# State-space scan on Trainium2: the first state of three scans in four is carried by ScalarE in place of a pointer

## The chip, the cores and the metric

The kernel runs on one core of a Trainium2 chip. The metric is the device time of one execution in microseconds (us). A core has five engines that run side by side, each with a queue of its own that it works off in order: TensorE (PE in the profile; its weight loads are PEld), VectorE (DVE), ScalarE (ACT), GpSimd (POOL) and SyncE (SP), which here only issues DMAs. An engine waits for another through semaphores, and while an instruction waits, everything behind it in that queue waits too.

## The reference

There are two layers. The first is a Mamba block over 4 images of 128 channels and 128 x 128 pixels, read as sequences of 16384 tokens. A small MLP and a projection give 256 inner channels, a causal convolution and SiLU give `u`, and then the selective scan runs over the sequence with 16 states for each channel:

```
delta = softplus(dt @ dt_proj_w.T + dt_proj_b)
A = -exp(A_log)
def step(h, inp):
    d_t, B_t, C_t, u_t = inp
    dA = exp(d_t[:, :, None] * A)
    h = h * dA + d_t[:, :, None] * B_t[:, None, :] * u_t[:, :, None]
    y = einsum('bds,bs->bd', h, C_t)
    return (h, y)
_, ys = scan(step, h0, xs)          # h0 = 0
y = ys + u * D
y = y * silu(z)
```

An output projection, a group norm, SiLU and a residual follow. The second layer normalizes the result, forms four weights for each image, and filters the image in the frequency domain (real FFTs as products with constant matrices).

## The kernel before

`block0` is the first layer and takes nine tenths of the time. The four images are cut into 128 chunks of T = 512 tokens, 32 an image (`NCH`). Of a chunk, 256 channels x 16 states are 4096 recurrences of 512 steps. They are laid on the 128 partitions as 32 tiles of 128 x 512: two halves of the channels (`j`), four rounds of states (`r`), and four places (`p`). I call the four tiles of one (`j`, `r`) a group; a chunk has eight groups (`u`), and two slots for each, 16 slots a chunk (`NP`). Slot 2u has places 0 and 1 of its group, slot 2u+1 places 2 and 3.

For each tile the work is:

- ScalarE: `da = exp(delta * A)` (`exps`, line 393). The result of place 0 lies in SBUF in two buffers, that of places 1, 2 and 3 in one PSUM bank each, so the next group's exponential of a place has to wait until VectorE is done with this one's.
- GpSimd: `hb = du * B` for places 1 to 3 (`dbu`, line 363), issued two slots ahead. For place 0, TensorE transposes a product of ScalarE into PSUM (`b0`, line 383).
- VectorE: the scan `h = da * h + b` over 512 steps (`scans`, line 412). Its first state is a constant 0 in the first chunk of an image; otherwise it is read through a pointer, a [128,1] column `st` that holds the last state of the chunk before.
- h*C: for places 2 and 3 VectorE multiplies (line 414), and ScalarE then copies the last column to `st` (line 415). For places 0 and 1 GpSimd multiplies (line 419), and ScalarE copies the last columns one slot later (phase "late", reported as line 554). `by_vector` has the exceptions: one tile more goes to VectorE in odd chunks, one less in "norming" chunks.
- TensorE: the sum over states into `y` (`sums`, line 433).

The order is written out by hand. Every step is put into a list under a slot and a phase (`todo`), and a loop over slots and phases issues them, so that each engine's queue follows the order of the phases. In one odd slot, ScalarE's queue is: place 1's exponential, the late state copy, the chunk's other work (phase "act"), the early exponential of place 0 of the group after, and the state copies of the scans. In the even slot it is: the exponentials of places 2 and 3, then other work. That other work is the preparation of the next chunks: Relu, copies, SiLU with a table load at slot 2 (lines 242 and 239), softplus with two table loads at slot 6 (line 275), the scaling of `bt` (line 304), and so on.

From image 1 on, the work of finishing the image before is spread over the chunks: chunks 2 to 17 of an image (`norming`) normalize (lines 633, 637 and 641), the later ones form the aggregation (line 667), and `spectrum` computes parts of the FFT ahead of time in some chunks. `spectrum` has one-buffer tiles: `fx` for the loaded rows, `fs` between the two products and `fq` for the stored result.

`block1` is the second layer. The change doesn't touch it.

Of the kernel before, what the change touches and what calls it, by code (L numbers as in the profile page):

```python
# [26 lines left out]
F32 = mybir.dt.float32  # L27
AF = mybir.ActivationFunctionType
# [5 lines left out]
P = 128  # L34
# [3 lines left out]
NP = 16  # L38
# [8 lines left out]
def kernel(ctx: ExitStack, tc: tile.TileContext, a: dict, out: bass.AP):  # L47
# [101 lines left out]
    spec = [dpool.tile([H, C, 2, WF], F32, tag=f"spec_{b}", name=f"spec_{b}") for b in range(EARLY)]  # L149
    shared = SimpleNamespace(**{k: v for k, v in locals().items() if k not in ("ctx", "tc")})  # L150
    block0(tc, shared)
    block1(tc, shared)


def block0(tc, s):
    nc, B, NCH, NH, NS, NG, ND, R, NX, KC, HALO, C, L, NF, DI = (
        s.nc, s.B, s.NCH, s.NH, s.NS, s.NG, s.ND, s.R, s.NX, s.KC, s.HALO, s.C, s.L, s.NF, s.DI,
    )
    NT = T // P
    with ExitStack() as ctx:  # L160
        def pool(name, bufs, **kw):
            return ctx.enter_context(tc.tile_pool(name=name, bufs=bufs, **kw))

        p1 = pool("p1", 1)
        p2 = pool("p2", 2)
        hpool = pool("hb", 4)
        tiny = pool("tiny", 2)
# [13 lines left out]
        st = {}  # L181
# [156 lines left out]
        def norming(k):  # L338

            return k >= NCH and 2 <= k % NCH < 2 + NCH // 2  # L340

        def place(r, p):


            return (p - r) % ND

        def by_vector(k, j, r, p):

            if norming(k):
                return p > 1 and (j, r, p) != (1, 2, 2)  # L350
            return p > 1 or (k % 2 == 1 and (j, r, p) == (1, 2, 1))

        def dbu(u):

# [13 lines left out]
        def pair(n):  # L368

            k, r = divmod(n, NP)  # L370
            u, p = divmod(r, ND // 2)
            j, r = divmod(u, NG)
            return k, j, r, 2 * p
# [11 lines left out]
        def exps(n, qs):  # L385
# [3 lines left out]
            for q in qs:  # L389
# [3 lines left out]
                nc.scalar.activation(da, d["delta", j][:, m, :], AF.Exp, scale=s.amat[:, c : c + 1])  # L393
                d["da", j, r, p + q] = da

        def scans(n):


            k, j, r, p = pair(n)
            d = st[k]  # L400
            hb = d["hb", j, r]
            das = [d.pop(("da", j, r, p + q)) for q in range(2)]
            dve = [q for q in range(2) if by_vector(k, j, r, p + q)]
            pool = [q for q in range(2) if q not in dve]
            last = d["last", j, r, p] = tiny.tile([P, 2], F32, tag=f"st{j}_{r}_{p}", name=f"st_{k}_{j}_{r}_{p}")
            if pool:
                h = p2.tile([P, 2, T], F32, tag="h", name=f"h_{k}_{j}_{r}_{p}", bufs=3)
            for q in range(2):
                b = hb[:, p + q, :] if p + q else d.pop("b0")
                init = 0.0 if k % NCH == 0 else st[k - 1]["last", j, r, p][:, q : q + 1]  # L410
                o = das[q] if q in dve else h[:, q, :]
                nc.vector.tensor_tensor_scan(o, das[q], b, init, ALU.mult, ALU.add)  # L412
            for q in dve:
                nc.vector.tensor_tensor(hb[:, p + q, :], das[q], d["C"][:, p + q, :], ALU.mult)  # L414
                nc.scalar.copy(last[:, q : q + 1], das[q][:, T - 1 : T])  # L415
            if pool:
                q = slice(pool[0], pool[-1] + 1)
                ps = slice(p + pool[0], p + pool[-1] + 1)
                nc.gpsimd.tensor_tensor(hb[:, ps, :], h[:, q, :], d["C"][:, ps, :], ALU.mult)  # L419
                todo[n + 1, "late"].append(partial(nc.scalar.copy, last[:, q], h[:, q, T - 1]))  # L420
# [47 lines left out]
        def spectrum(b, c0, n):  # L468

            g = {}  # L470

            def load():
                g["x"] = p1.tile([s.H, 3, s.W], F32, tag="fx", name=f"fx_{b}_{c0}")
                nc.sync.dma_start(out=g["x"][:, 0:n], in_=s.x1[b][c0 : c0 + n].rearrange("c h w -> h c w"))

            def over_h():
                g["pa"] = psp.tile([s.W, 3, 2 * s.WF], F32, tag="pp", name=f"pp_fa_{b}_{c0}")
                for q in range(n):
                    nc.tensor.matmul(g["pa"][:, q], g["x"][:, q], s.fh, start=True, stop=True)

            def evict():
                g["sa"] = p1.tile([s.W, 3, 2 * s.WF], F32, tag="fs", name=f"fs_{b}_{c0}")
                nc.scalar.copy(g["sa"][:, 0:n], g["pa"][:, 0:n])

            def over_w():
                half = s.H // 2
                g["px"] = psp.tile([s.H, 3, 2 * s.WF], F32, tag="pp", name=f"pp_fx_{b}_{c0}")
                for q in range(n):
                    re, im = g["sa"][:, q, 0 : s.WF], g["sa"][:, q, s.WF :]
                    for (data, a, b_), start in (((re, s.fwr, s.fwr), True), ((im, s.fwi, s.fwm), False)):  # L490
                        for at, w in ((0, a), (1, b_)):
                            o = g["px"][at * half : (at + 1) * half, q]
                            nc.tensor.matmul(o, data[:, at : at + half], w, start=start, stop=not start)

            def store():
                x = p1.tile([s.H, 3, 2, s.WF], F32, tag="fq", name=f"fq_{b}_{c0}")
                nc.scalar.copy(x[:, 0:n].rearrange("h c r k -> h c (r k)"), g["px"][:, 0:n])  # L497
                nc.sync.dma_start(out=s.spec[b][:, c0 : c0 + n], in_=x[:, 0:n])

            return [  # L500
                (4, "pe", load), (12, "pe", over_h), (12, "end", evict), (13, "pe", over_w), (13, "end", store),
            ]

        n_chunks = B * NCH
        todo = defaultdict(list)
# [33 lines left out]
        for n in range(n_chunks * NP):  # L539
            if n % 2 == 0:  # L540
                todo[n - 3, "early"].append(partial(exps, n, (0,)))
            todo[n - 1, "exps"].append(partial(exps, n, (1,) if n % 2 == 0 else (0, 1)))
            todo[n - 1, "turn"].append(partial(dbu_turn, n))
            todo[n, "scans"].append(partial(scans, n))
            if n % 2 == 0:
                todo[n - 2, "dbu"].append(partial(dbu, n // 2))
            else:
                todo[n + 2, "sums"].append(partial(sums, n // 2))
        slots = [n for n, _ in todo]
        with tc.manual_schedule():  # L550
            for n in range(min(slots), max(slots) + 1):
                for phase in ("turn", "sums", "pe", "exps", "late", "act", "pool", "dbu", "early", "gate", "scans", "dve", "end"):
                    for f in todo[n, phase]:
                        f()

# [503 lines left out]
```

## Time and profile before

| what | us |
|---|---|
| median of 3 runs | 7132.03 (7131.95 to 7132.24) |
| the profiled execution | 7134.96 |
| its span, first to last instruction | 7133.1 |
| first layer: last scan starts at | 6409.8 |
| VectorE scans (line 412) with a pointer, 3968 of them | 1214 to 1293 ns each |
| VectorE h*C (line 414), x2040 | 674 ns mean |
| GpSimd du*B (line 363) and h*C (line 419) | 3604.8 and 2434.0 busy |
| ScalarE exponentials (line 393), x4096 | 2794.1 busy, 700 ns mean |
| ScalarE idle before line 415, for VectorE's line 414 | 471.4 |

In the page, each engine's busy time stands with its share of the span, and groups of instructions with their number, busy time and mean duration. Instructions of one engine overlap a little at their ends, so the time from one start to the next is shorter than the duration. In the timeline a row "x2" joins two that follow each other; its length less one duration is the time from start to start.

### The profile page before, as it was taken

The numbers are of one execution on the slowest core, as the hardware profiler recorded it, in microseconds if no ns is written. First come the engines' busy times: TensorE is split into PE (matmuls) and PEld (weight loads), VectorE is DVE, ScalarE is ACT, GpSimd is POOL, SyncE is SP. The second block draws the span as 40 slices with busy tenths as digits, with TensorE's granted clock in tenths as the row PEclk, the third lists the DMA queues.
The fourth block names the chain that finished last, engine by engine and source line by source line (L and its number), as shares of the span: only waits on it lengthen the run. The fifth ranks groups of instructions, "written<-read, shape, count | busy, mean of one in ns | idle before, by whom it ended". The sixth has DMA issues, their size and how long they took to land.

```text
span 7133.1 us, 91388 instructions
## 1 busy us (share of the span) xinstructions
PE 5887.2 (83%) x26708; PEld 2606.0 (37%) x26708; DVE 6888.6 (97%) x7966; ACT 6140.8 (86%) x13658; POOL 6892.0 (97%) x3188
## 2 busy tenths in 40 slices
PE   6888888888887788888888888888888888877899
PEld 2333333323222233333333333333333333326789
DVE  6999999999999999999999999999999999997888
ACT  6888888888888888898888888898888888877887
POOL 6999999999999999999999999999999999997898
PEclk8888888888888889998898899998889899989999
DMA  6666666667777776777777777677777767759977
GB/s 140 159 154 162 159 151 164 160 151 176 180 188 182 182 172 170 180 180 172 195 186 196 188 175 178 168 187 173 197 189 195 190 167 177 172 140 271 274 213 209
DMA packets 909640, 1288.33 MB, mean 181 GB/s; under 512 B 81736, under 2 KB 360912, under 8 KB 909136
## 3 DMA queue, kind: packets, MB, share of 16 engines
q1 hardware_dynamic: 908992, 1282.22, 72.4%
q8 instruction: 210, 3.44, 0.2%
q14 instruction: 294, 2.41, 0.1%
q10 hardware_dynamic: 144, 0.26, 0.0%
HBM read 1025.58 MB, written 256.58 MB: 180 GB/s over the span
## 4 chain that ended last, share of the span: by engine, by line
DVE 44%; ACT 30%; issue 11%; PE 6%; DMA 4%; POOL 3%; SPq 1%; DVEq 0%; ACTq 0%; POOLq 0%
DVE da L412 20%; DVE h L412 12%; ACT da L393 12%; DVE hb L414 5%; ACT L393 3%; DMA rdelta<-dd 2%; ACT L275 2%; ACT delta L275 2%; ACT bt L304 2%; PE y L433 1%; DVE zs L443 1%; POOL hb L363 1%; ACT L242 1%; DVE pr L894 1%; POOL hb L419 1%
## 5 line engine op out<-in xcount | busy, mean ns | idle before, releaser
L363 POOL TENSOR_TENSOR hb<-rdu,rB 128x1536 f32<-128x1536 f32 (+2 forms) x1536 | 3604.8, 2363 | 22.4 <-DMA rdelta<-dd 21.3
L393 ACT ACTIVATE da<-rdelta,amat 128x512 f32<-128x512 f32 x4096 | 2794.1, 700 | 138.3 <-DVE h L412 133.9
L419 POOL TENSOR_TENSOR hb<-h,rC 128x1024 f32<-128x1024 f32 (+1 forms) x1072 | 2434.0, 2273 | 89.1 <-DVE h L412 73.8
L412 DVE TENSOR_TENSOR_SCAN da<-da,st,hb 128x512 f32<-128x512 f32 x1976 | 2419.9, 1267 | 21.4 <-ACT da L393 14.3
L433 PE MATMUL y<-hb,sel 128*32 128x512 f32 x8192 | 1314.2, 717 | 2.9 <-POOL hb L419 2.7
L414 DVE TENSOR_TENSOR hb<-da,rC 128x512 f32<-128x512 f32 x2040 | 1296.3, 674 | 3.0
L412 DVE TENSOR_TENSOR_SCAN h<-da,st,b 128x512 f32<-128x512 f32 x992 | 1258.4, 1269 | 1.8 <-PE b L383 1.6
L412 DVE TENSOR_TENSOR_SCAN h<-da,st,hb 128x512 f32<-128x512 f32 x1000 | 1251.8, 1256 | 1.8 <-ACT da L393 1.8
L383 PE MATMUL b<-ident,bt 128*128 128x128 f32 x4096 | 747.3, 305 | 517.1 <-DVE h L412 391.7
L234 PE MATMUL pp_cv<-xm,wck 128*128 128x512 f32 x2048 | 1013.5, 640 | 1.6 <-ACT xm L217 0.8
L304 ACT ACTIVATE bt<-pt_dut,xdt 128x256 f32<-128x256 f32 x2048 | 839.4, 474 | 184.5 <-PE pt_dut L293 184.3
L383 PEld LDWEIGHTS b<-ident,bt 128*128 128x128 f32 x4096 | 530.8, 154 | 1017.6 <-DVE h L412 691.6
L415 ACT COPY st<-da 128x1 f32<-128x1 f32 x2040 | 273.2, 160 | 474.5 <-DVE hb L414 471.4
L234 PEld LDWEIGHTS pp_cv<-xm,wck 128*128 128x128 f32 x2048 | 395.5, 203 | 651.9 <-issue 422.5
L830 POOL TENSOR_TENSOR wb<-wb,term 128x1040 f32<-128x1040 f32 x192 | 461.3, 2403 | 39.0 <-ACT term L824 29.6
L293 PE MATMUL pt_dut<-ident,du 128*128 128x128 f32 x1024 | 232.1, 337 | 287.7 <-ACT xdt L286 176.3
L429 PE MATMUL y<-u,diag 128*128 128x512 f32 x512 | 303.0, 675 | 187.6 <-DVE zs L443 186.1
L293 PEld LDWEIGHTS pt_dut<-ident,du 128*128 128x128 f32 x1024 | 131.9, 162 | 606.9 <-POOL du L312 478.4
L393 ACT ACT_TABLE_LOAD x262 | 336.1, 1283 | 12.0 <-DMA rdelta<-dd 7.4
L312 POOL TENSOR_TENSOR du<-delta,u 128x512 f32<-128x512 f32 x256 | 318.7, 1266 | 28.1 <-ACT delta L275 28.1
L223 PE MATMUL pp_z<-xm,win 128*128 128x512 f32 x512 | 274.5, 634 | 51.8 <-ACT fq L497 46.2
L267 PE MATMUL pp_dt<-xd,wdt 8*128 8x512 f32 x512 | 284.9, 641 | 33.2 <-ACT pp_o L457 23.5
(160 smaller groups left out, 8095.7 us busy)
## 6 DMA issues: line engine op xcount, KB each, us to landing
rdelta<-dd SPq DMA_DIRECT2D x1024, 256.0 KB, 4.6
rdu<-dd SPq DMA_DIRECT2D x1024, 256.0 KB, 7.4
rC<-bc SPq DMA_DIRECT2D x512, 256.0 KB, 7.4
rB<-bc SPq DMA_DIRECT2D x512, 192.0 KB, 4.7
dd<-delta SPq DMA_DIRECT2D x256, 256.0 KB, 7.2
dd<-du SPq DMA_DIRECT2D x256, 256.0 KB, 5.7
ft<-in_filt_w SPq DMA_DIRECT2D x108, 520.0 KB, 7.2
ob<-o SPq DMA_DIRECT2D x128, 256.0 KB, 2.1
```

The source lines that it names most:

```text
L234: nc.tensor.matmul(ps["cv", j], w, d["xm"][:, t : t + T], start=t == 0, stop=t == KC - 1)
L293: nc.tensor.transpose(ps["dut"][:, 2 * t + j, :], d["du"][:, j, at : at + P], s.ident)
L304: nc.scalar.activation(d["bt"][:, 2 * h + t, :, q, :], src, AF.Copy, scale=d["xdt"][:, 2 * h + t, R + q : R + q + 1])
L312: nc.gpsimd.tensor_tensor(du, d["delta"][:, j, :], d["u"][:, j, :], ALU.mult)
L363: nc.gpsimd.tensor_tensor(hb[:, p : p + n, :], d["du", j][:, m : m + n, :], d["B"][:, p - 1 : p - 1 + n, :], ALU.mult)
L383: nc.tensor.transpose(b[:, t * P : (t + 1) * P], src, s.ident)
L393: nc.scalar.activation(da, d["delta", j][:, m, :], AF.Exp, scale=s.amat[:, c : c + 1])
L412: nc.vector.tensor_tensor_scan(o, das[q], b, init, ALU.mult, ALU.add)
L414: nc.vector.tensor_tensor(hb[:, p + q, :], das[q], d["C"][:, p + q, :], ALU.mult)
L419: nc.gpsimd.tensor_tensor(hb[:, ps, :], h[:, q, :], d["C"][:, ps, :], ALU.mult)
L433: nc.tensor.matmul(y[m * DG : (m + 1) * DG, :], s.sel, d["hb", j, r][:, p, :], start=False, stop=r == NG - 1)
L830: nc.gpsimd.tensor_tensor(wb, wb, u[n].terms[f], ALU.add)
```

## The change

Places 1 to 3 of every group scan from the constant 0 in every chunk. To make up for it, the state carried from the chunk before is added to the first column of `du*B`: the recurrence's first step is da * h_last + b, so b's first column becomes exp(delta_0 * A) * h_last + b. ScalarE does this with one ACTIVATE (Identity) on one column for each place, 24 a chunk (`carries`), whose scale is the last state and whose bias is the column itself, both read through pointers. The factors exp(delta_0 * A) come from four small exponentials of 128 x 4 for each half, 8 a chunk (`decays`). First chunks of an image have neither. Place 0 keeps its pointer.

`by_vector` now gives VectorE places 2 and 3 in all chunks, and the tile (1, 2, 1) in all that aren't "norming": one tile more than before in 40 plain even chunks and in 48 norming ones. GpSimd has that tile less.

`spectrum` works in one tile: rows, intermediate and result overwrite one another.

```diff
         def by_vector(k, j, r, p):
             if norming(k):
-                return p > 1 and (j, r, p) != (1, 2, 2)
-            return p > 1 or (k % 2 == 1 and (j, r, p) == (1, 2, 1))
+                return p > 1
+            return p > 1 or (j, r, p) == (1, 2, 1)
...
+        def decays(k, j):
+            d = st[k]
+            e = d["e", j] = tiny.tile([P, NG, ND], F32, tag=f"e{j}", name=f"e_{k}_{j}")
+            a = s.amat.rearrange("p (j g m) -> p j g m", j=NH, m=ND)
+            for m in range(ND):
+                nc.scalar.activation(e[:, :, m], a[:, j, :, m], AF.Exp, scale=d["delta", j][:, m, 0:1])
+
+        def carries(u):
+            k, r = divmod(u, NH * NG)
+            j, r = divmod(r, NG)
+            if k % NCH:
+                for p in range(1, NG):
+                    first = st[k]["hb", j, r][:, p, 0:1]
+                    last = st[k - 1]["last", j, r, p - p % 2][:, p % 2 : p % 2 + 1]
+                    m = place(r, p)
+                    nc.scalar.activation(
+                        first, st[k]["e", j][:, p, m : m + 1], AF.Identity, scale=last, bias=first
+                    )
...
-                init = 0.0 if k % NCH == 0 else st[k - 1]["last", j, r, p][:, q : q + 1]
+                init = 0.0 if p + q or k % NCH == 0 else st[k - 1]["last", j, r, p][:, q : q + 1]
                 o = das[q] if q in dve else h[:, q, :]
                 nc.vector.tensor_tensor_scan(o, das[q], b, init, ALU.mult, ALU.add)
...
             def load():
-                g["x"] = p1.tile([s.H, 3, s.W], F32, tag="fx", name=f"fx_{b}_{c0}")
+                g["f"] = p1.tile([s.H, 3, 2 * s.WF], F32, tag="fx", name=f"fx_{b}_{c0}")
...
             def evict():
-                g["sa"] = p1.tile([s.W, 3, 2 * s.WF], F32, tag="fs", name=f"fs_{b}_{c0}")
-                nc.scalar.copy(g["sa"][:, 0:n], g["pa"][:, 0:n])
+                nc.scalar.copy(g["f"][:, 0:n], g["pa"][:, 0:n])
...
             if n % 2 == 0:
                 todo[n - 2, "dbu"].append(partial(dbu, n // 2))
-            else:
+                todo[n - 1, "carry"].append(partial(carries, n // 2))
+            if n % (2 * NG) == 0 and n // NP % NCH:
+                todo[n - 3, "decay"].append(partial(decays, n // NP, n // (2 * NG) % NH))
+            if n % 2:
                 todo[n + 2, "sums"].append(partial(sums, n // 2))
...
-                for phase in ("turn", "sums", "pe", "exps", "late", "act", "pool", "dbu", "early", "gate", "scans", "dve", "end"):
+                for phase in ("turn", "sums", "pe", "exps", "late", "act", "pool", "dbu", "carry", "early", "decay", "gate", "scans", "dve", "end"):
```

So in ScalarE's queue the carries of group u stand in slot 2u-1, after the chunk's other work and before place 0's early exponential. The decays stand in slots 5 and 13, after the early exponential.

More of the change, by code (lines that the diff above doesn't have):

```diff
@@ L472, in load @@
             def load():
-                g["x"] = p1.tile([s.H, 3, s.W], F32, tag="fx", name=f"fx_{b}_{c0}")
-                nc.sync.dma_start(out=g["x"][:, 0:n], in_=s.x1[b][c0 : c0 + n].rearrange("c h w -> h c w"))
+                g["f"] = p1.tile([s.H, 3, 2 * s.WF], F32, tag="fx", name=f"fx_{b}_{c0}")
+                nc.sync.dma_start(out=g["f"][:, 0:n, 0 : s.W], in_=s.x1[b][c0 : c0 + n].rearrange("c h w -> h c w"))
             def over_h():
@@ L478, in over_h @@
                 for q in range(n):
-                    nc.tensor.matmul(g["pa"][:, q], g["x"][:, q], s.fh, start=True, stop=True)
+                    nc.tensor.matmul(g["pa"][:, q], g["f"][:, q, 0 : s.W], s.fh, start=True, stop=True)
             def evict():
-                g["sa"] = p1.tile([s.W, 3, 2 * s.WF], F32, tag="fs", name=f"fs_{b}_{c0}")
-                nc.scalar.copy(g["sa"][:, 0:n], g["pa"][:, 0:n])
+                nc.scalar.copy(g["f"][:, 0:n], g["pa"][:, 0:n])
             def over_w():
@@ L488, in over_w @@
                 for q in range(n):
-                    re, im = g["sa"][:, q, 0 : s.WF], g["sa"][:, q, s.WF :]
+                    re, im = g["f"][:, q, 0 : s.WF], g["f"][:, q, s.WF :]
                     for (data, a, b_), start in (((re, s.fwr, s.fwr), True), ((im, s.fwi, s.fwm), False)):
@@ L495, in store @@
             def store():
-                x = p1.tile([s.H, 3, 2, s.WF], F32, tag="fq", name=f"fq_{b}_{c0}")
-                nc.scalar.copy(x[:, 0:n].rearrange("h c r k -> h c (r k)"), g["px"][:, 0:n])
+                nc.scalar.copy(g["f"][:, 0:n], g["px"][:, 0:n])
+                x = g["f"].rearrange("h c (r k) -> h c r k", r=2)
                 nc.sync.dma_start(out=s.spec[b][:, c0 : c0 + n], in_=x[:, 0:n])
```

## The prediction

> **What bounds the kernel now.** I read the page first (busy time by engine, the costliest groups), then the busy time of each engine in four single chunks (one each of the plain stretch, of the two kinds with normalization, and of the stretch with aggregation), then the scans with their shapes kept apart, then the timeline of ScalarE and VectorE over two groups.
>
> ```profile
> PE 5887.2 (83%) x26708; PEld 2606.0 (37%) x26708; DVE 6888.6 (97%) x7966; ACT 6140.8 (86%) x13658; POOL 6892.0 (97%) x3188
> ...
> 558.02:606.39 48.37, 39.62 (x152) 14.69 (x152) 48.37 (x51) 41.71 (x93) 47.51 (x22) 0.89 0.69 159
> 2031.13:2081.43 50.30, 38.88 (x150) 13.82 (x149) 50.27 (x55) 43.25 (x95) 50.05 (x24) 0.86 0.73 184
> 3524.38:3574.68 50.30, 40.74 (x183) 16.11 (x182) 50.27 (x55) 43.94 (x97) 50.09 (x24) 0.90 0.79 192
> 4277.85:4326.97 49.12, 42.26 (x188) 17.24 (x187) 49.09 (x53) 43.94 (x100) 48.67 (x23) 0.93 0.72 179
> ```
>
> The columns of the second view are the stretch, its length, and the busy time of PE, PEld, DVE, ACT and POOL. VectorE is busy in all 48.37 us of a plain chunk, so the chunk lasts as long as VectorE's work. GpSimd has 1% left, ScalarE 6.7 us.
>
> ```profile
> L412 DVE TENSOR_TENSOR_SCAN da<-da,st,hb x1976: 1214/1266/1293, 121.2 to 6409.8; 128x512 f32<-128x512 f32 x198
> L412 DVE TENSOR_TENSOR_SCAN h<-da,st,hb x1000: 1245/1256/1284, 120.0 to 6407.5; 128x512 f32<-128x512 f32 x167
> ...
> L412 DVE TENSOR_TENSOR_SCAN da<-da,hb x64: 1169/1206/1232, 56.9 to 4861.4; 128x512 f32<-128x512 f32 x64
> ...
> L412 DVE TENSOR_TENSOR_SCAN h<-da,hb x32: 1190/1196/1224, 55.8 to 4859.2; 128x512 f32<-128x512 f32 x32
> ...
> 1626.84 2.44 DVE L412 TENSOR_TENSOR_SCAN da<-da,st,hb 128x512 f32<-128x512 f32 x2
> ...
> 1632.61 2.32 DVE L412 TENSOR_TENSOR_SCAN da<-da,hb 128x512 f32<-128x512 f32 x2
> ```
>
> The first chunk of each image already scans from the constant 0 (no "st" among the inputs), so the trace prices the change: 1266 to 1206 ns and 1256 to 1196 ns. Two such scans take 2.32 us in place of 2.44, which is 60 ns each from start to start as well.
>
> ```profile
> 558.20 1.31 ACT L393 ACTIVATE da<-rdelta,amat 128x512 f32<-128x512 f32 x2
> ...
> 564.10 1.31 ACT L393 ACTIVATE da<-rdelta,amat 128x512 f32<-128x512 f32 x2
> 565.42 1.28 ACT L242 ACT_TABLE_LOAD   x1
> ...
> 571.74 1.30 ACT L393 ACTIVATE da<-rdelta,amat 128x512 f32<-128x512 f32 x2
> ...
> 576.48 1.31 ACT L393 ACTIVATE da<-rdelta,amat 128x512 f32<-128x512 f32 x2
> ...
> 566.86 2.46 DVE L412 TENSOR_TENSOR_SCAN da<-da,st,hb 128x512 f32<-128x512 f32 x2
> ...
> 572.78 2.44 DVE L412 TENSOR_TENSOR_SCAN da<-da,st,hb 128x512 f32<-128x512 f32 x2
> ...
> 2041.92 1.48 ACT L633 ACTIVATE pp_n<-of,bias,scale 128x512 f32<-128x512 f32 x2
> ...
> L580 ACT ACTIVATE mv<-mv,q x4: 294/294/295, 1702.7 to 6437.8; 128x1 f32<-128x1 f32 x4
> ```
>
> The "x2" rows of line 393 are the exponentials of places 2 and 3 of groups 0, 1, 2 and 3 of a chunk. I call the time from one such pair to the next a segment. They take 5.90, 7.64 and 4.74 us. The long one holds the Silu work and two table loads. Place 2's exponential of group 1 ends at 564.79 and its scan starts at 566.86: a slack of 2.07 us. In group 2 it ends at 572.43 and its scan starts at 572.78: a slack of 0.35. So ScalarE, though idle for 6.7 us of the chunk, is 0.35 us from stopping VectorE after its heaviest segment.
>
> **What the Trainium skill says.** "ScalarE: Activation LUTs", section "What ACT_TABLE_LOAD costs": an ACTIVATE takes 186 ns and 0.833 ns for each element, about 93 ns more for each [128,1] pointer operand, and back-to-back ones overlap by about 93 ns. The trace agrees: line 580 (one element, one pointer) has 294 ns against 280; the two-pointer line 633 mean 779 against 799, and its x2 row (1.48 less 0.78) is 0.70 from start to start. The section "Table sets: the hidden batching unit" says that cheap functions lie in every set; the trace has the Identity of line 620 between exponentials without a load. "VectorE: DVE Perf Modes", section "Scalar operands", says that a scalar is a constant or a [P,1] operand, but gives no price; the scans above do.
>
> **The change, part by part.**
>
> *Scans.* 24 of a chunk's 32 scans lose the pointer: 24 x 0.0605 = 1.45 us of VectorE, in 124 chunks (first chunks of images have no pointer now) 180 us.
>
> *One more h*C on VectorE.* It joins in 40 plain even chunks and 48 normalizing ones: 0.59 us each from start to start (two in 1.27), 52 us in all. GpSimd loses 1.09 us (a half of a pair) or 1.23 us (one alone): 104 us. The extra state copy on ScalarE (0.05) is left out. VectorE's chunk becomes 47.5 us plain (48.37 + 0.59 - 1.45) and 49.4 normalizing. GpSimd's is 47.7 and 48.8. If nothing else were added, some 115 us would go.
>
> *Carries.* 24 one-element ACTIVATEs a chunk, with both scale and bias by pointer, reading SBUF. The trace doesn't show this one. From line 633: 0.705 start to start less 511 x 0.833 ns = 0.28 us. The page's price gives the same (186 + 186 + 1 - 93 = 280). From below, the copies of line 415 (no pointer) follow each other by 0.04 to 0.06. From above, the dependent one-element pair of lines 588 and 589 by 0.32. I take 0.279: 0.84 us a group, 6.7 a chunk.
>
> *Decays.* 8 Exps of 128x4 a chunk, scale by pointer: 186 + 93 + 3 - 93 = 0.19; I take 0.2 (line 691, of this size, lasts 297 ns less the overlap). 0.8 us each in the segments after groups 2 and 6, beside exponentials, so no table load.
>
> *Waits.* A carry waits for GpSimd's du*B, behind it on ScalarE stand place 0's next exponential, two state copies and the next pair of exponentials. In the timeline GpSimd's product ends 1.4 to 5.1 us before the scan of place 1 (in nearly all groups), and GpSimd gets slacker, so I price this wait at nothing; uncovered, it would be up to 1 us in some groups.
>
> *Spectrum tile.* The in-place tile makes the next load wait for the last store. The store lands 1.9 us after issue; the next load is issued 6.5 us later (2971.62 to 2978.07) and read eight slots on. Nothing; if not, SP holds 2 us inside a slack of some 20.
>
> **The sum.** ScalarE's work in the eight segments of a plain chunk is, from the timeline, 2.69, 7.60, 4.35, 6.85, 4.47, 5.25, 4.83, 4.71 us (40.8; the busy 41.71 has the tails before its gaps). With 0.84 each, and 0.8 more in the third and seventh, it is 49.2, against 47.5 of VectorE: ScalarE becomes the bound. Segment by segment: slack at the next group = slack + VectorE's time (5.72, and 6.30 where it also gates or has the extra product) - ScalarE's segment; below nothing VectorE stops. A segment can't be shorter than 4.3 us + slack, since place 2's and 3's state copies wait for the products (4.74 less 0.35 in the trace, less two pointers). With old numbers this rule returns 48.38 us and the slacks 2.07, 0.35 to 0.6 and 1.5. With new ones: 2.0 after group 0; the segment of 8.44 stops VectorE for 0.71 us; 5.99 for 0.27; 7.69 (softplus, two loads) for 1.97; the rest fits. The chunk lasts 50.5 us. With normalization the Silu segment has 2.4 us more on VectorE too: 51.7 in image 1, 52.5 in images 2 and 3 (aggregation of the image before adds 0.7 on ScalarE). In plain chunks with aggregation, ScalarE has 1.3 and 0.7 us more in two segments: 51.9.
>
> Against now: 31 x (50.5 - 48.75) = 53; 16 x (51.7 - 50.3) = 23; 32 x (52.5 - 50.3) = 69; 41 x (51.9 - 49.0) = 121; three chunks at stage borders 3 each. Sum +275 us. The profiled execution, 7134.96 (span 7133.1), becomes 7410; on the median of 7132.03 that is 7407.
>
> **Rivals.** The measurement tells about 0.2% from no change.
> - Carries cost one pointer's price, 0.2 each (the two reads overlap): the same rule gives +130, 7262. For it: line 580's 294 ns. Against it: line 633. Chance 0.17.
> - Carries follow each other by 0.32 or more, or ScalarE also waits for GpSimd, some 3 us a chunk in the end: +380, 7510. For it: lines 588 and 589; against it: the carries don't depend on each other. Chance 0.2.
> - The pointer-free scan saves nothing after a ScalarE write: +340, 7470. Against it: the four scan rows. Chance 0.05.
> - Other side: the carries pipeline like the state copies, 0.06 each, and ScalarE stays inside its idle time: VectorE's 47.9 and 49.3 us decide, -110, 7022. It decides from a carry under 0.14 us. For it: two copies of line 415 in 0.21 us; against it: these have no pointer. Chance 0.08; at 0.12 to 0.16 nothing would be seen, 0.03.
>
> The forecast has 0.47. Range 7265 to 7512, which takes in the one-pointer case and the serial one nearly. Faster 0.08, same 0.03, slower 0.89.
>
> **What would show it.** Right: ScalarE busy above 97% in the chunks, VectorE idle about 2.5 us before scans of place 2 with ScalarE's exponential as releaser, GpSimd idle; the scans at 1206 and 1196 ns; the carry 373 ns long and 0.28 from start to start. Wrong: a carry well under 0.2, or VectorE still at 99% in the plain chunks.

## The result and the profile after

The changed kernel takes 7529.69 us (median of 4 runs, 7526.68 to 7530.66) against 7131.99 for the kernel before on the same chip: a ratio of 1.0557, 95% interval 1.0545 to 1.057. The loss is 397 us. I had predicted 275, and the measured time lies 18 us above my range.

The page of the changed kernel, busy time by engine and the share of each engine in the chain that ended last:

```profile
PE 5951.8 (79%) x26708; PEld 2653.5 (35%) x26708; DVE 6843.0 (91%) x8054; ACT 7102.1 (94%) x17666; POOL 6802.2 (90%) x3140
...
ACT 60%; PE 17%; DVE 10%; issue 5%; DMA 5%; SPq 2%; POOL 0%; ACTq 0%; DVEq 0%; POOLq 0%
```

The same chain in the kernel before:

```profile
DVE 44%; ACT 30%; issue 11%; PE 6%; DMA 4%; POOL 3%; SPq 1%; DVEq 0%; ACTq 0%; POOLq 0%
```

VectorE and ScalarE have changed places: ScalarE is busy for 961 us more (6140.8 before), and carries 60% of the chain. TensorE's share of the chain goes from 6% to 17% with the same number of matmuls. The second fact points to what the prediction lacked.

One chunk from each of four stages of the changed kernel (plain, normalizing in image 1, normalizing in image 3, aggregating). Columns: stretch, length, busy time of PE, PEld, DVE, ACT and POOL, clock, DMA share and rate:

```profile
577.47:628.67 51.20, 38.20 (x156) 14.48 (x152) 48.31 (x53) 49.68 (x127) 47.91 (x23) 0.90 0.67 151
2124.22:2176.36 52.14, 39.35 (x156) 14.46 (x152) 49.76 (x56) 50.92 (x128) 48.90 (x23) 0.86 0.74 177
3718.89:3771.53 52.64, 41.94 (x186) 16.66 (x182) 49.67 (x56) 51.49 (x130) 49.11 (x23) 0.86 0.76 182
4885.26:4937.52 52.26, 40.59 (x186) 16.07 (x184) 48.37 (x53) 51.32 (x132) 47.93 (x23) 0.95 0.73 169
```

ScalarE's column is now the fullest everywhere: 97% of the plain chunk. Over whole stages, the chunks at their borders left out, the mean chunk went from 48.75 to 51.16 us (plain), 50.33 to 52.53 (normalizing, image 1), 50.34 to 53.03 (normalizing, images 2 and 3) and 48.98 to 53.13 (aggregating).

The costly groups of the changed kernel; behind the second bar stands the idle time of the engine just before them, and what ended most of it:

```profile
L440 POOL TENSOR_TENSOR hb<-h,rC 128x1024 f32<-128x1024 f32 (+1 forms) x1024 | 2329.9, 2275 | 524.4 <-DVE h L433 513.8
...
L433 DVE TENSOR_TENSOR_SCAN da<-da,hb 128x512 f32<-128x512 f32 x2128 | 2490.6, 1214 | 283.0 <-ACT da L393 222.1
...
L433 DVE TENSOR_TENSOR_SCAN h<-da,hb 128x512 f32<-128x512 f32 x944 | 1134.8, 1202 | 168.6 <-ACT hb L413 161.8
...
L413 ACT ACTIVATE hb<-e,hb,st 128x1 f32<-128x1 f32 x2976 | 938.0, 387 | 0.1
```

The scans without a pointer last 1214 and 1202 ns, so the saving on VectorE is there. But VectorE sits idle 283.0 us before the scans in the `da` row, which are mostly those of places 2 and 3 (222.1 of it for ScalarE's exponential), and 168.6 us before those of place 1 in the `h` row (161.8 of it for the carry). GpSimd, with less work than before, waits 513.8 us for VectorE's scans. The carries themselves wait for nothing (0.1 us in all): ScalarE never stands still for GpSimd's product.

ScalarE's timeline over two peaks of the plain chunk from 577.47 on (start, length, engine, line; x2 or x3 joins rows that follow each other; in brackets the engine's idle time just before, and what ended it):

```profile
583.35 1.31 ACT L393 ACTIVATE da<-rdelta,amat 128x512 f32<-128x512 f32 x2
584.67 1.28 ACT L242 ACT_TABLE_LOAD   x1
585.97 1.06 ACT L242 ACTIVATE zs<-zs 128x1024 f32<-128x1024 f32 x1
586.93 0.67 ACT L239 ACTIVATE u<-pp_cv,conv_b 128x512 f32<-128x512 f32 x1
587.92 0.69 ACT L239 ACTIVATE u<-pp_cv,conv_b 128x512 f32<-128x512 f32 x1 [0.32 <-PE pp_cv L234]
588.62 1.28 ACT L393 ACT_TABLE_LOAD   x1
...
590.63 0.94 ACT L413 ACTIVATE hb<-e,hb,st 128x1 f32<-128x1 f32 x3
...
592.25 1.30 ACT L393 ACTIVATE da<-rdelta,amat 128x512 f32<-128x512 f32 x2
...
604.33 0.94 ACT L413 ACTIVATE hb<-e,hb,st 128x1 f32<-128x1 f32 x3
605.17 0.71 ACT L393 ACTIVATE da<-rdelta,amat 128x512 f32<-128x512 f32 x1
605.79 0.19 ACT L436 COPY st<-da 128x1 f32<-128x1 f32 x2
605.96 1.30 ACT L393 ACTIVATE da<-rdelta,amat 128x512 f32<-128x512 f32 x2
```

And VectorE's timeline at the same places:

```profile
591.05 1.22 DVE L433 TENSOR_TENSOR_SCAN h<-da,hb 128x512 f32<-128x512 f32 x1 [0.16 <-ACT hb L413]
593.03 2.35 DVE L433 TENSOR_TENSOR_SCAN da<-da,hb 128x512 f32<-128x512 f32 x2 [0.77 <-ACT da L393]
...
604.75 1.22 DVE L433 TENSOR_TENSOR_SCAN h<-da,hb 128x512 f32<-128x512 f32 x1 [1.07 <-ACT hb L413]
606.68 2.35 DVE L433 TENSOR_TENSOR_SCAN da<-da,hb 128x512 f32<-128x512 f32 x2 [0.71 <-ACT da L393]
```

From one exponential pair to the next (583.35 to 592.25) is 8.90 us: the Silu segment, predicted at 8.44. The three carries take 0.94 us as a row; less one duration of 0.387 and halved, that is 0.28 from start to start (278 ns is the median of the run). At 587.92 ScalarE waits 0.32 us for TensorE's convolution. Then place 1's scan stops for the carry, and place 2's for the exponential behind it, 0.93 us together, and after the softplus segment 1.78 us.

### The profile page after: what moved, and what is told of

It is laid out like the page before. It is cut to its first block, busy times and chain, and to the rows that moved or that the text cites. A ratio compares the mean times of both kernels' runs of the same rounds, so it can differ in the third digit from the quotient of the medians.

```text
span 7528.6 us, 94424 instructions
## 1 busy us (share of the span) xinstructions
PE 5951.8 (79%) x26708; PEld 2653.5 (35%) x26708; DVE 6843.0 (91%) x8054; ACT 7102.1 (94%) x17666; POOL 6802.2 (90%) x3140
## 4 chain that ended last, share of the span: by engine, by line
ACT 60%; PE 17%; DVE 10%; issue 5%; DMA 5%; SPq 2%; POOL 0%; ACTq 0%; DVEq 0%; POOLq 0%
ACT da L393 20%; ACT hb L413 8%; PE pp_cv L234 7%; ACT bt L304 7%; PE y L454 4%; ACT L393 4%; DVE da L433 3%; ACT e L402 2%; ACT L275 2%; ACT delta L275 2%; DVE h L433 2%; DMA rdu<-dd 2%; PE y L450 2%; DVE hb L435 2%; DMA rdelta<-dd 1%
## 5 line engine op out<-in xcount | busy, mean ns | idle before, releaser
L440 POOL TENSOR_TENSOR hb<-h,rC 128x1024 f32<-128x1024 f32 (+1 forms) x1024 | 2329.9, 2275 | 524.4 <-DVE h L433 513.8
L433 DVE TENSOR_TENSOR_SCAN da<-da,hb 128x512 f32<-128x512 f32 x2128 | 2490.6, 1214 | 283.0 <-ACT da L393 222.1
L435 DVE TENSOR_TENSOR hb<-da,rC 128x512 f32<-128x512 f32 x2128 | 1351.8, 675 | 2.8
L454 PE MATMUL y<-hb,sel 128*32 128x512 f32 x8192 | 1335.5, 729 | 4.5 <-POOL hb L440 3.0
L433 DVE TENSOR_TENSOR_SCAN h<-da,hb 128x512 f32<-128x512 f32 x944 | 1134.8, 1202 | 168.6 <-ACT hb L413 161.8
L234 PE MATMUL pp_cv<-xm,wck 128*128 128x512 f32 x2048 | 1045.8, 657 | 1.4 <-ACT xm L217 0.8
L413 ACT ACTIVATE hb<-e,hb,st 128x1 f32<-128x1 f32 x2976 | 938.0, 387 | 0.1
L223 PE MATMUL pp_z<-xm,win 128*128 128x512 f32 x512 | 293.8, 672 | 145.7 <-ACT fx L516 139.9
L436 ACT COPY st<-da 128x1 f32<-128x1 f32 x2128 | 239.6, 159 | 124.0 <-DVE hb L435 123.3
```

Of the source, the lines that this page charges most:

```text
L234: nc.tensor.matmul(ps["cv", j], w, d["xm"][:, t : t + T], start=t == 0, stop=t == KC - 1)
L413: nc.scalar.activation(first, st[k]["e", j][:, p, m : m + 1], AF.Identity, scale=last, bias=first)
L454: nc.tensor.matmul(y[m * DG : (m + 1) * DG, :], s.sel, d["hb", j, r][:, p, :], start=False, stop=r == NG - 1)
```

## The experiments

Ratios are to the kernel before, with their 95% intervals. An edit is against the changed kernel unless another is named.

### Each part alone

The h*C tile moved, in the kernel before:

```diff
-                return p > 1 and (j, r, p) != (1, 2, 2)
-            return p > 1 or (k % 2 == 1 and (j, r, p) == (1, 2, 1))
+                return p > 1
+            return p > 1 or (j, r, p) == (1, 2, 1)
```

> The kernel before with the h*C tile moved to VectorE and nothing else. Theory A: VectorE, the bound, gets 88 times 0.59 us: 7165 to 7190. Rival (GpSimd is as much the bound, so its relief pays): 7100 to 7140.

Measured: 7175.47 us, 1.006 (1.0045 to 1.0075), as expected. By itself the tile costs 44 us over 88 chunks, near the 52 of the prediction.

The in-place tile of the spectrum, in the kernel before:

```diff
...
-                g["sa"] = p1.tile([s.W, 3, 2 * s.WF], F32, tag="fs", name=f"fs_{b}_{c0}")
-                nc.scalar.copy(g["sa"][:, 0:n], g["pa"][:, 0:n])
+                nc.scalar.copy(g["f"][:, 0:n], g["pa"][:, 0:n])
...
```

> The kernel before with the in-place spectrum tile and nothing else. The prediction's price: nothing, within 10 us of the kernel before. Rival: the load waits for the store and holds the other loads on its queue, 20 us or more.

Measured: 7132.98 us, 1.0002 (0.9993 to 1.001). It is no part of the loss.

The changed kernel without carries and without decays, so that everything is left but ScalarE's new work:

```diff
-                todo[n - 1, "carry"].append(partial(carries, n // 2))
-            if n % (2 * NG) == 0 and n // NP % NCH:
-                todo[n - 3, "decay"].append(partial(decays, n // NP, n // (2 * NG) % NH))
```

> The changed kernel without the carries and the decays; it leaves out what places 1 to 3 carry from one chunk to the next. Theory A (ScalarE's occupied time is the whole cost): VectorE and GpSimd are the bound again, plain chunks 47.5 to 47.8 us, normalizing ones 49.4, total 6990 to 7030. Theory C (the in-place spectrum tile or the moved product costs too): over 7060.

Measured: 6997.63 us, 0.9811 (0.9782 to 0.9839). The plain chunk is 47.69 us, with VectorE busy for 47.64 of it. So the scans and the tile together are worth -135 us (I had said some -115), and ScalarE's new instructions cost 532 us, all of the loss and more.

### How the loss grows with ScalarE's work

The decays alone (no carries):

```diff
-                todo[n - 1, "carry"].append(partial(carries, n // 2))
```

> The changed kernel with the decays but without the carries (it leaves out what places 1 to 3 carry from chunk to chunk). Theory A: 1.5 us more of ScalarE a chunk, in two segments with room, costs next to nothing against the run without both (6998): 6995 to 7030. Rival (ScalarE has no room at all): 7080 or more.

The carry with no pointer, and with one:

```diff
-                    nc.scalar.activation(
-                        first, st[k]["e", j][:, p, m : m + 1], AF.Identity, scale=last, bias=first
-                    )
+                    nc.scalar.activation(first, first, AF.Identity)
```

> The carries stay, at the same places and with the same waits for GpSimd and by VectorE, but without scale and bias pointers (the column is copied onto itself, so the carry itself is left out). Theory A: each holds ScalarE for about 0.11 us in place of 0.28, and the segment rule gives 7080 to 7160. Theory B (the hand-over from GpSimd through ScalarE's queue to VectorE is the cost): most of the loss stays, over 7350.

```diff
-                    nc.scalar.activation(
-                        first, st[k]["e", j][:, p, m : m + 1], AF.Identity, scale=last, bias=first
-                    )
+                    nc.scalar.activation(first, first, AF.Identity, scale=last)
```

> The carries keep the scale pointer and lose the bias (the sum is left out). Theory A: 0.19 us each, 7230 to 7310, between the run without pointers and the full change, with steps in proportion to 0.09 us x 2976. Theory B: no difference from the full change, 7500 or more.

| ScalarE's extra | one, start to start (ns) | added per chunk (us) | time (us) | ratio, interval | step (us) |
|---|---|---|---|---|---|
| none | | 0 | 6997.63 | 0.9811 (0.9782 to 0.9839) | |
| 8 decays | 191 | 1.5 | 7067.02 | 0.9908 (0.9888 to 0.9928) | 69 |
| and 24 carries, no pointer | 93 | 2.2 | 7183.04 | 1.0071 (1.0048 to 1.0094) | 116 |
| one pointer | 185 | 2.2 | 7338.32 | 1.0288 (1.0259 to 1.0318) | 155 |
| two pointers (the change) | 278 | 2.2 | 7529.69 | 1.0557 (1.0545 to 1.057) | 191 |

All three runs came out above what I expected, by 37, 23 and 28 us. The prices of single instructions are right: a pointer adds 92 to 93 ns, as the Trainium skill states ("ScalarE: Activation LUTs", section "What ACT_TABLE_LOAD costs"). But three equal steps of 2.2 us a chunk cost 116, 155 and 191 us: over 124 chunks that is 0.42, 0.56 and 0.69 us of time for each us of work. The fuller ScalarE is, the more of each further us reaches the end. And the decays were not hidden, as the run without carries shows. ScalarE's and VectorE's timelines of that run, in a plain chunk:

```profile
570.09 0.87 ACT L402 ACTIVATE e<-amat,rdelta 128x4 f32<-128x4 f32 x4
...
571.03 1.30 ACT L393 ACTIVATE da<-rdelta,amat 128x512 f32<-128x512 f32 x2
572.35 1.28 ACT L275 ACT_TABLE_LOAD   x1
```

```profile
578.64 2.34 DVE L433 TENSOR_TENSOR_SCAN da<-da,hb 128x512 f32<-128x512 f32 x2 [0.41 <-ACT da L393]
```

The decays stand between the Silu segment and the softplus segment, the short stretch in which ScalarE can regain its lead before the next peak. It enters the softplus peak with a slack of 0.67 us (1.33 without the decays), and VectorE stops for 0.41 us behind it, although in that chunk ScalarE is idle for about 5 us elsewhere.

### Place against total

Six carries a chunk instead of 24, the other groups with the old pointer: once those of groups 2 and 4, which stand in the two peaks, once those of groups 1 and 6, which stand where ScalarE has room:

```diff
-            if k % NCH:
+            if k % NCH and u % 8 in (2, 4):
...
-                init = 0.0 if p + q or k % NCH == 0 else st[k - 1]["last", j, r, p][:, q : q + 1]
+                zero = p + q and NG * j + r in (2, 4)
+                init = 0.0 if zero or k % NCH == 0 else st[k - 1]["last", j, r, p][:, q : q + 1]
```

> The changed kernel with carries for groups 2 and 4 of a chunk alone, whose carries stand in ScalarE's heaviest segments; the other groups keep the pointer. All eight decays stay. Theory S (what counts is where ScalarE's extra stands, since VectorE has 2 us of slack at most to bridge a heavy segment): the segment rule gives 7260, with its shortfall up to 7300. Theory T (what counts is ScalarE's total a chunk, 3.2 us more of the 6.7 idle): the same as the run with groups 1 and 6.

The second has (1, 6) in both places.

> As the run before, with groups 1 and 6 in place of 2 and 4: as many carries, as many scans without a pointer, in light segments. Theory S: the rule gives 7120, with its shortfall 7120 to 7165, at least 100 us under the other. Theory T: within 20 us of the other.

Measured: 7322.19 us, 1.0268 (1.0253 to 1.0283), and 7191.80 us, 1.0085 (1.007 to 1.01). ScalarE is busy for the same time in both, 6510.7 and 6512.0 us. The 130 us between them are those of place alone (the rule of the prediction gives 140), so ScalarE's total isn't what counts alone. Both times lie above what I expected, by 22 and 27 us, and above the rule's own figures by 62 and 72: the rule had the right shape and lacked a term that depends little on place.

### The missing term: TensorE

What ScalarE waits for (in all, times, longest), in the kernel before:

```profile
ACT st L415 <- DVE hb L414: 471.4, 800, 11.6
ACT bt L304 <- PE pt_dut L293: 184.3, 142, 3.5
ACT da L393 <- DVE h L412: 133.9, 163, 3.2
...
ACT u L239 <- PE pp_cv L234: 10.6, 6, 4.9
```

and in the changed kernel:

```profile
ACT st L436 <- DVE hb L435: 123.3, 269, 13.1
...
ACT bt L304 <- PE pt_dut L293: 56.1, 105, 3.7
ACT u L239 <- PE pp_cv L234: 42.3, 61, 2.7
...
ACT pt_agg L690 <- PE pt_agg L686: 18.2, 11, 2.8
```

The waits for VectorE shrink to a quarter, as they should when ScalarE is late. Of those for TensorE, the largest shrinks too, to a third (line 304), but the one for the convolution grows fourfold, and what is left of them now stands in the queue that sets the end. TensorE's timeline tells why the convolution comes late. In a plain chunk of the kernel before:

```profile
554.78 0.33 PE L383 MATMUL b<-ident,bt 128*128 128x128 f32 x1 [0.78 <-ACT bt L304]
...
562.75 3.70 PE L234 MATMUL pp_cv<-xm,wck 128*128 128x512 f32 x8
```

and of the changed kernel:

```profile
575.77 0.48 PE L383 MATMUL b<-ident,bt 128*128 128x128 f32 x1 [2.18 <-ACT bt L304]
...
584.18 3.70 PE L234 MATMUL pp_cv<-xm,wck 128*128 128x512 f32 x8
```

A transpose for place 0 waits for ScalarE's `bt`, 0.78 us before and 2.18 now, and the sums and the convolution stand behind it. The convolution ends 2.35 us after the start of group 1's exponential pair in the kernel before (566.45 against 564.10), and 4.53 in the changed one (587.88 against 583.35), where ScalarE is ready for it 0.3 us sooner. So a late ScalarE makes TensorE late, and TensorE hands it back. To test what this costs, the convolution with one of its four taps in the changed kernel, and as a control in the kernel before:

```diff
-                for t in range(KC):
+                for t in range(KC - 1, KC):
...
-                    nc.tensor.matmul(ps["cv", j], w, d["xm"][:, t : t + T], start=t == 0, stop=t == KC - 1)
+                    nc.tensor.matmul(ps["cv", j], w, d["xm"][:, t : t + T], start=True, stop=True)
```

> The changed kernel with one of the convolution's four matmuls for each half (the other three taps are left out), which frees TensorE of 3.8 us a chunk. Theory P (a late ScalarE makes TensorE late, and TensorE hands it back; this is what the prediction missed): 7430 to 7480, 50 to 100 us under the changed kernel. Rival (the missing 120 us are ScalarE's own work): within 20 us of 7530.

> The kernel before with the same three taps left out, as a control. Theory P: VectorE is the bound and TensorE has slack, so within 20 us of 7132. Rival (the taps cost the kernel before as much): 50 us or more under 7132.

Measured: 7490.23 us, 1.0501 (1.048 to 1.0522), so 39 us less than with four taps, where I had expected 50 to 100; the control 7160.54 us, 1.0039 (1.0023 to 1.0055), 28 us more than before, which I hadn't expected either. In the changed kernel the wait of line 239 is gone, the Silu segment takes 8.48 us (8.44 predicted), and the plain chunk takes 50.78 on the mean, 0.38 less than with four taps.

By stage, the normalizing chunks of image 1 are 0.57 us shorter (51.96), those of images 2 and 3 0.44 (52.59), the aggregating ones only 0.15 (52.98). The control's own loss isn't in the normalizing chunks, which keep their 50.3 us. A lower clock of TensorE isn't the cause in the plain chunks: the mean granted clock there was 0.90 in the changed kernel, 0.86 in the kernel before and 0.83 in the one-tap kernel without the wait.

The trace of the changed kernel with all taps gives the wait the same price: its first plain chunk, in which ScalarE doesn't wait for the convolution yet, takes 50.78 us; over the next seven the wait grows to 0.32 us and the chunk to 51.19, where both stay. In the normalizing chunks of image 1 it is 51.96 us in those without the wait and up to 53.36 in those with one of 1.3 us.

The opposite attempt, the second half of the convolution one slot earlier, so that ScalarE finds it done:

```diff
-                (0, "pe", partial(cv_mm, 0)), (1, "pe", partial(cv_mm, 1)), (2, "act", silu_act),
+                (0, "pe", partial(cv_mm, 0)), (0, "pe", partial(cv_mm, 1)), (2, "act", silu_act),
```

> The changed kernel with the second half of the convolution's matmuls issued one slot earlier on TensorE. In the changed kernel ScalarE waits 42 us for these matmuls before its Silu. Theory P (TensorE, itself held up behind late ScalarE, gives part of the loss back to ScalarE): this wait goes and the time falls by 20 to 40 us, to 7490 to 7510. Rival: the wait turns into one of VectorE for the transposed place 0, which now stands behind the matmuls: within 15 us of 7530 or above.

Measured: 7701.88 us, 1.08 (1.0782 to 1.0818), worse by 172 us than the changed kernel. TensorE's transposes for place 0 now stand behind eight more matmuls (a half of the convolution, in the profile's count), and VectorE waits for them, 59.4 us in all in the changed kernel and here:

```profile
DVE h L433 <- PE b L383: 387.5, 128, 37.5
```

The wait of line 239 is gone, as meant, but TensorE has no free place in that slot either: the rival of that expectation was right.

### The carry on another engine

On VectorE: one product of 128 x 12 for a half, and one sum of 128 x 3 for each group, in place of ScalarE's carries (the product isn't shown).

```diff
...
-                for p in range(1, NG):
-                    first = st[k]["hb", j, r][:, p, 0:1]
...
-                    nc.scalar.activation(
-                        first, st[k]["e", j][:, p, m : m + 1], AF.Identity, scale=last, bias=first
-                    )
+                first = st[k]["hb", j, r][:, 1:ND, 0]
+                nc.vector.tensor_tensor(first, first, st[k]["g", j][:, r, :], ALU.add)
...
```

> The carry done on VectorE: one product of decay and last state for each half of a chunk, one add of three columns for each group, issued before the scans of the group; ScalarE keeps the eight decays. Theory A: VectorE pays some 0.06 to 0.1 us a group for 0.18 saved, so 7040 to 7090, under both kernels. Rival: the small adds hold VectorE for 0.15 or more each, or wait for GpSimd's product just before the scan of place 0; then 7130 to 7250.

Measured: 8291.95 us, 1.1626 (1.1592 to 1.1659): the largest miss of the study. The sum of three columns, in VectorE's timeline, against GpSimd's at the same time:

```profile
568.27 0.15 DVE L422 TENSOR_TENSOR hb<-hb,g 128x3 f32<-128x3 f32 x1
...
574.14 2.51 DVE L422 TENSOR_TENSOR hb<-hb,g 128x3 f32<-128x3 f32 x1
...
595.48 2.57 DVE L422 TENSOR_TENSOR hb<-hb,g 128x3 f32<-128x3 f32 x1
```

```profile
564.39 3.44 POOL L363 TENSOR_TENSOR hb<-rdu,rB 128x1536 f32<-128x1536 f32 x1
...
573.19 3.44 POOL L363 TENSOR_TENSOR hb<-rdu,rB 128x1536 f32<-128x1536 f32 x1
...
594.60 3.42 POOL L363 TENSOR_TENSOR hb<-rdu,rB 128x1536 f32<-128x1536 f32 x1
```

At 568.27 GpSimd has just ended (567.83), and the sum lasts 0.15 us. At 574.14 GpSimd is in the middle of a product that ends at 576.63; the sum ends at 576.65. At 595.48 the product ends at 598.02, the sum at 598.05. The Trainium skill says that "A DVE instruction with two SBUF inputs contends with a GpSimd instruction that reads SBUF", and calls the port pair that the two share an exclusive lock ("SBUF — State Buffer", section "Who interferes with whom"). The trace agrees to 0.03 us. A rival is that the sum merely waits for the product it adds to. The same trace speaks against it: of the 992 sums, 916 start while a GpSimd instruction runs, and every one of them ends 16 to 29 ns after that instruction, also the 246 beside an instruction whose result the sum doesn't read (lines 312 and 449). The scans and multiplications beside GpSimd keep their durations; each has an operand in PSUM.

On GpSimd, with one more h*C tile on VectorE to make room (the product and that tile aren't shown):

```diff
...
+                nc.gpsimd.tensor_tensor(first, first, st[k]["g", j][:, r, :], ALU.add)
...
-                todo[n - 1, "carry"].append(partial(carries, n // 2))
+                todo[n - 2, "dbu"].append(partial(carries, n // 2))
...
```

> The carry done on GpSimd (one product of 12 columns for each half of a chunk, one add of three columns for each group right behind the product du*B), the decays on ScalarE, and one h*C tile more on VectorE to make room on GpSimd. If GpSimd's small operations cost the 0.14 us that its sizes of 512, 1024 and 1536 have in common, both engines have 48.1 to 48.3 us a plain chunk and 50.0 a normalizing one: 7060 to 7110, under both kernels. Rival: a small GpSimd operation behind the one that it depends on costs 0.3 us or more, or GpSimd waits for the decays; then 7130 to 7300.

The same with the sum one place later in GpSimd's queue, behind the h*C of the group before:

```diff
-                todo[n - 2, "dbu"].append(partial(carries, n // 2))
+                todo[n - 1, "pool"].append(partial(carries, n // 2))
```

> The carry on GpSimd as in the run before, but with the add one place later in GpSimd's queue, behind the h*C of the group before, so that it doesn't follow the product it depends on. In the run before each add had 0.2 us and 0.08 us idle ahead of it. Theory: 0.1 us a group less on GpSimd, 7080 to 7130, under the kernel before. Rival: the add now comes just when VectorE needs it in the groups where GpSimd is late, VectorE waits, 7160 or more.

Measured: 7165.39 us, 1.0048 (1.0032 to 1.0064), and 7390.77 us, 1.0359 (1.0342 to 1.0376). Both missed the range that I expected and lie in the rival's. The first is 364 us under the changed kernel, but not under the kernel before: the sum lasts 198 ns, and GpSimd is idle some 0.08 us ahead of each. In the second VectorE waits 244.5 us for it.

### A form that fits into ScalarE's room

b's first column need not change. If the first column of da is multiplied by the last state and the scan starts from the constant 1, the first step is da_0 * h_last * 1 + b_0, the same value. That takes one ACTIVATE with one pointer and no decays. I gave it to 14 of 32 tiles a chunk, none of them in the peaks:

```diff
...
+            return u in (0, 1, 3, 5, 6, 7) if p == 1 else p > 1 and u in (0, 5, 6, 7)
...
+                    first = st[k]["da", j, r, p + q][:, 0:1]
+                    last = st[k - 1]["last", j, r, p][:, q : q + 1]
+                    nc.scalar.activation(first, first, AF.Identity, scale=last)
...
+                init = 1.0 if by_one(k, NG * j + r, p + q) else 0.0 if k % NCH == 0 else st[k - 1]["last", j, r, p][:, q : q + 1]
...
```

> The kernel before with another carry: ScalarE multiplies the first column of the decay tile by the last state, in place, and the scan starts from the constant 1, so no decays and no wait for GpSimd are needed. One pointer, some 0.18 us. Only for 14 of 32 tiles a chunk, all outside the heavy segments; the h*C tile as in the changed kernel, but in normalizing chunks for even ones alone. Theory S: VectorE 48.1 us in a plain chunk and 49.75 in a normalizing one, 7060 to 7100, under both kernels. Rival: the in-place column on the exponential just before it makes ScalarE wait, and late segments lose it again: 7130 or more.

Measured: 7129.53 us, 0.9993 (0.9985 to 1.0002): no change, 30 us above the range that I expected. The operation takes 144 ns from start to start. Plain chunks gained 14 us in all and normalizing ones 16, aggregating ones lost 9, and the rest lost 18. Then the same without the aggregating chunks, which keep the old pointer and the old split of tiles:

```diff
-            if k % NCH == 0:
+            if k % NCH == 0 or aggregating(k):
                 return False
...
```

> As the run before it (e16), but in the chunks that aggregate the old pointer and the old split of tiles are kept. In e16 the first state by ScalarE's scaling shortened a plain chunk by 0.46 us and a normalizing one by 0.27 to 0.5 us, and made an aggregating one 0.24 us longer. If these are independent of each other, 31 x 0.46 + 48 x 0.33 = 30 us stay, less some 5 for the chunks at the stage borders: 7095 to 7115, under both kernels. Rival: the gain of the plain chunks is taken back by waits at the borders and in the other chunks, as in e16, and the time stays within 15 us of the kernel before (7117 to 7147).

Measured: 7109.12 us, 0.9968 (0.9955 to 0.998), within the range that I expected, 0.3% under the kernel before and 5.6% under the changed one. Its busy times:

```profile
PE 5908.6 (83%) x26708; PEld 2623.3 (37%) x26708; DVE 6851.7 (96%) x8006; ACT 6293.8 (89%) x14780; POOL 6847.8 (96%) x3164
```

VectorE is the fullest again, with 37 us less work than before, of which 22 reach the time. ScalarE has 153 us more to do, and they are hidden.

## Why the prediction was right in direction and 122 us short

*Scans.* Right: 1214 and 1202 ns in the changed kernel, where 1206 and 1196 were forecast.

*Tile and scans together.* -135 us measured with nothing else added, -115 predicted.

*Carries and decays.* Right in price: 278 against 279 ns, 191 against 200. The one-pointer rival and the rival of the other side fall with this, and so does the serial one: at 7510 us it named a time near the measured one, but its mechanism isn't there. The carries follow each other by 278 ns, not 320, and wait 0.1 us in all for GpSimd, which I had priced at nothing. The rival that the scan saves nothing falls by the scans' rows.

*Spectrum tile.* Nothing, as predicted.

*What would show it.* ScalarE is at 97%, GpSimd idle, and VectorE idles 2.9 us in a plain chunk (the mean over 24 of them), where the rule had 0.71 + 0.27 + 1.97 = 2.95. Of that a part stands before place 1 with the carry as releaser, 161.8 us against 222.1 with the exponential; I had named only the second. That 2.9 and 2.95 agree so well is in part luck. The rule counts a stop from when the scan could have started; idle time counts from the end of the instruction before. With the overlap that is lost at the stops (0.5 us a chunk, last section), the stops of the rule measure 3.4 us.

*The step that failed* is the rule in "The sum". In it ScalarE is held up by VectorE alone; its waits for TensorE are put at nothing. The largest of them in the profile before, 184 us for line 304, stood in idle time, and I left it out as if it would vanish with that idle time. Two thirds of it did, 56 us stayed. The wait for the convolution, 10.6 us before, grew to 42.3, because TensorE itself waits for a late ScalarE, and on the path such waits count. Segment by segment in the plain chunk this can be read: the segments predicted at 8.44, 5.99 and 7.69 us measure 8.87, 5.99 and 7.72 on the mean, and 0.28 of the first is the wait for the convolution. In the aggregating chunks ScalarE waits for line 304 (12.9 us over 38 chunks), line 690 (10.7) and line 239 (6.2). The chunks there in which it waits for none of them take 52.0 to 52.3 us, near the 51.9 predicted, while the mean is 53.13 and those with a wait at line 690 take 55.4 to 56.6.

By comparison with the chunks without such waits, TensorE accounts for 31 x 0.38 in the plain chunks, 16 x 0.57 and some 32 x 0.5 in the normalizing ones, and 41 x 1.0 in the aggregating ones: 78 of the 122 us. Of the 37 in the plain and normalizing chunks, taking taps away removes some 33, so these are shown. Of the 41 in the aggregating chunks it removes 6; the rest stands at lines 304 and 690, is read from the trace only, and its removal wasn't tried. There the granted clock was lower too (0.90 on the mean against 0.94 before), and what of TensorE's lateness comes from that stays open. Some 15 more are the chunks at the stage borders and the first ones of an image, which I had at 9 and lost 23. The rest is in sums of 0.02 to 0.3 us a chunk that I can't take apart. Two slips in the sums of the prediction don't matter here: ScalarE's segments add up to 49.1 us, not 49.2, and its stages hold 123 of the 124 chunks, which leaves out some 3 us. The control has a loss of its own, so a comparison of the two one-tap kernels (330 us between them, not 397) would give TensorE 67 us instead of 39 for the convolution; which is nearer stays open.

## What to carry to other kernels

Before giving work to an engine with idle time, look at where in the period that idle time lies: work in a peak, or in the stretch in which the engine recovers between two peaks, reaches the end long before the engine is full. And when an engine is to become the bound, go through every wait in its row of the profile, those for third engines too, and ask what each becomes when this engine is late. A wait that costs nothing inside idle time can stay in part when the idle time is used up, and a small one can grow, when the third engine waits for this one in its turn. A cheaper form of the same step, placed only where there is room, gained 0.3% where the full one lost 5.6%.

## What I hadn't expected of the hardware

A VectorE sum of 128 x 3 with both inputs in SBUF lasted 0.15 us with GpSimd idle and up to 2.86 us beside GpSimd's products, 1379 ns on the mean of 992.

A stop costs more than its idle time. In a plain chunk of the changed kernel VectorE's instructions overlap each other by 3.74 us in all, against 4.24 in the one without carries and decays: with 6 stops more, 0.08 us for each.

With three quarters of the convolution's matmuls left out, the kernel before got 28 us slower: its granted clock was 0.857 against about 0.90, and ScalarE waits for TensorE at lines where it hardly waited before (39.5 us at line 456 and 26.0 at line 253, against 4.6 and 1.2). Why the clock is lower with less work these runs don't show.
